# Reversed order inside each group of an attention context's products

## The chip, the cores and the metric

The kernel runs on one core of a Trainium2 chip. The metric is the device time of one execution in microseconds (us). A profile of one execution stands beside the timed runs; its "span" reaches from the first to the last instruction that the profiler recorded, and the execution's own time is a little longer than its span.

Engines are named as in the profile: PE is TensorE's matrix multiplier and PEld its weight load, DVE is VectorE, ACT is ScalarE, POOL is GpSimd, and SP is the engine whose queue starts most transfers. L597 means line 597 of the kernel.

## The reference

For each of 16 batches, x is 512 channels by 1024 tokens, and the mask `cond_2048` holds 0 or 1 per token.

```python
xt = jnp.transpose(x, (0, 2, 1))
q = xt @ Wq.T
qh = q.reshape(B, T, NH, dk).transpose(0, 2, 1, 3)          # 8 heads of 64
scores = scale * jnp.einsum('bhqd,bhkd->bhqk', qh, qh)
logits = (scores * cmask + (1.0 - cmask) * NEG) * rmask
attn = jax.nn.softmax(logits, axis=-1)
ctx = jnp.einsum('bhqk,bhkd->bhqd', attn, qh)
out = ctx.transpose(0, 2, 1, 3).reshape(B, T, D) @ Wo.T
return x + jnp.transpose(out, (0, 2, 1))
```

Queries, keys and values are the same projection. A token with mask 0 is left out as a key; as a query its logits are all zero, so its row of the context is the mean over all tokens.

## The kernel before

**Slots.** About half of the tokens have mask 1. The kernel numbers the tokens of a batch so that those come first, and does attention on the first 544 slots alone: four blocks of 128 slots (i = 0 to 3) and a tail of 32 (i = 4). All other tokens get the mean row.

**A step.** A batch is worked off in 18 steps, in the order of the list `S`: for each head pair p = 0 to 3 and each block i = 0 to 3 one step, and two steps for the tails of four heads each (`None`). In a step (p, i) the function `scores` runs once per head k of the pair (L580): four f16 matmuls, keys of block i against all 544 queries, into a PSUM tile `pss` of which there are two. ACT takes the exponential (L584) into an SBUF tile `p` of 128 x 544 floats, and adds up the rows on its way; there are nine such tiles.

**The context's products.** `attend(b, p, i, ps)` multiplies the block's values by its exponentials and adds the product to the PSUM tile `pav` (L597). It goes over two halves g of the 544 columns and over the two heads k. Each product has 64 output rows, and the two heads lie on different halves of the array's columns and of `pav`'s partitions. The operands are float32, and the profile shows each such product as two matmul rows: 16 batches x 4 pairs x 4 blocks x 2 halves x 2 heads are 1024 products, and 2048 rows. The tail's product (L600) has all 128 output rows and closes the sum; then ACT copies `pav` out (L604), after which the next pair may use the only `pav` tile.

**Groups.** `attend` isn't called in the step of its exponentials. The lists `todo`, `ready` and `now` in `run` hold it back: blocks 0 and 1 of pair p come in step (p, 3), and blocks 2 and 3 in step (p+1, 1), for the last pair in step (0, 1) of the next batch, there with the tail behind them. Two blocks make a group of eight products, or 16 rows of L597. There are eight groups in a batch and 128 in all. Below they are counted from 0: group 0 of a batch is blocks 0 and 1 of pair 0, group 1 is blocks 2 and 3 of pair 0, and so on to group 7.

**What else PE does.** While a batch's attention runs, `run` spreads over its steps the transposes of the next batch's rows (L398), its projection (L421), its values (L467, L484), the row maxima (L509, L518), the transposes of the sums' reciprocals (L633), and the output projection of the batch before (L680). Each piece has a cost, and a step is given pieces until its share of the batch's total is reached. Where the first of them is dear, they are written ahead of the group in the same step, else behind it.

**What sets the order.** The order in which `run` writes the work is a priority and not the final order. When the program is built, a planner goes through all engines with an estimate of each instruction's time; on each engine it takes the first instruction, in the order written, whose operands and buffers are ready by its estimate. The order that comes out is fixed, and every engine then works its queue off in that order. The semaphore waits are added after that, and a wait is written only where the engine hasn't waited already for the same or a later point of the other engine.

Of the kernel before, what the change touches and what calls it, by code (L numbers as in the profile page):

```python
# [49 lines left out]
class Fast:  # L50
# [537 lines left out]

    def attend(self, b, p, i, ps):
        nc, s = self.nc, self.st[b]  # L590
        if i == 0:
            s["pav"] = self.ps_av.tile([P, 2, 512], F32, tag="av", name="pav")
        for g in range(2):
            for k in range(2):
                cols = slice(g * CH, (g + 1) * CH)
                if i < 4:
                    nc.tensor.matmul(s["pav"][k * DK:(k + 1) * DK, g, :CH], lhsT=s["v"][p][:, i, k * DK:(k + 1) * DK],  # L597
                                     rhs=ps[k][:, cols], start=(i == 0), stop=False)
                else:
                    nc.tensor.matmul(s["pav"][:, g, :CH], lhsT=s["vt"][p // 2][:, k, p % 2 * 2:p % 2 * 2 + 2, :],  # L600
                                     rhs=s["pt"][:, p % 2, cols], start=False, stop=(k == 1))
        if i == 4:
            c = self.sb([P, C], F32, "c", 3)
            nc.scalar.copy(c.rearrange("p (g c) -> p g c", g=2), s["pav"][:, :, :CH])  # L604
            s["c"].append(c)
# [194 lines left out]
    def run(self, flag):  # L800
# [80 lines left out]
        todo, ready, whole = [], [], []  # L881
        for b in range(B + 1):
# [64 lines left out]
            for st, (p, i) in enumerate(S):  # L947
                soon, self.soon = self.soon, []
                for f in soon + free.get(st, []):
                    f()  # L950
                if i is None:
                    self.scores(b, p, None)
                else:
                    ps = [self.scores(b, 2 * p, i)]
                    if i == 2 and whole:
                        whole.pop()()
                    ps.append(self.scores(b, 2 * p + 1, i))

                for _ in range(1 if b < B - 2 else -(-len(self.urgent + self.spare) // (N - st))):
                    self.issue()  # L960
                goal = total * (st + 1) / N
                fill = []
                while pos < len(m) and (done + m[pos][0] / 2 <= goal or st == N - 1):
                    fill.append(m[pos])
                    done += m[pos][0]
                    pos += 1

                big = st >= 4 and [c >= 1 for c, _ in fill if c > 0.1][:1] == [True]
                fill = [f for _, f in fill]

                now = []
                if i in (0, 2):
                    ready, todo = todo, []
                elif i in (1, 3):
                    now, ready = ready, []
                for f in fill + now if big else now + fill:
                    f()
                if i is not None:
                    todo.append(L(self.attend, b, p, i, ps))
                if i == 3:  # L980
                    (whole if p < 3 else todo).append(L(self.attend, b, p, 4, None))
                    if p < 3:
                        free.setdefault(st + 2, []).append(L(self.recip_sums, b, p))
                        free.setdefault(st + 3, []).append(L(self.recip_rows, b, p))
                        if p < 2 or b == B - 1:
                            free.setdefault(st + 5, []).append(L(self.norm, b, p))
# [148 lines left out]
```

## Time and profile before

| | |
|---|---|
| median of 3 runs | 1134.67 us (1131.85 to 1141.19) |
| profiled execution | 1133.56 us |
| its span | 1131.8 us |
| mean granted TensorE clock | 0.992 |
| PE busy | 1090.5 us, 96% |
| PEld busy | 707.9 us, 63% |
| DVE busy | 731.6 us, 65% |
| ACT busy | 676.2 us, 60% |
| POOL busy | 289.1 us, 26% |
| L597, the context's products | 2048 rows, 297.5 us busy |
| L584, the exponentials | 512, 363.3 us busy |

A busy time is the union of an engine's instructions. PE's matmuls overlap, and so the distance from the start of one to the start of the next says more than the duration of one. The idle column of a group of instructions gives the time in which the engine stood still just before them, and what released it.

### The profile page before, as it was taken

What the parts mean: (1) busy time and instruction counts of PE and PEld (TensorE: products, weight loads), DVE (VectorE), ACT (ScalarE), POOL (GpSimd) and SP (SyncE); (2) the same over time, 40 slices, a digit from 0 to 9 for tenths busy, and PEclk for the clock granted to TensorE, in tenths of its full rate; (3) what the DMA queues carried; (4) which work ended last, traced back from release to release, by engine and by line L of the source; (5) the groups of instructions that cost most, each with busy time, mean ns of one, the idle gap of its engine ahead of it and who ended that gap; (6) DMA issues with size and microseconds to landing.
All of it is one profiled execution on the core that took longest, in us unless ns stands there. A gap on an engine that the chain in (4) does not pass through costs nothing.

```text
span 1131.8 us, 23296 instructions
## 1 busy us (share of the span) xinstructions
PE 1090.5 (96%) x8386; PEld 707.9 (63%) x8386; DVE 731.6 (65%) x2369; ACT 676.2 (60%) x1716; POOL 289.1 (26%) x303
## 2 busy tenths in 40 slices
PE   7899999999999999999999999999999999998997
PEld 6566666666666666566666666566666666665543
DVE  6687567675665767667665666856576675655643
ACT  5776666666566666566565665666656566654540
POOL 3101021322202222222222232222222232214642
PEclk9899999999999999999999999999999999999999
DMA  6745554656546454655655566455655654545652
GB/s 212 218 117 151 143 159 128 191 142 179 149 127 175 124 201 137 171 175 158 189 150 165 154 177 185 129 181 144 195 166 156 188 152 130 149 126 174 204 161 77
DMA packets 78122, 181.35 MB, mean 160 GB/s; under 512 B 15008, under 2 KB 16800, under 8 KB 78000
## 3 DMA queue, kind: packets, MB, share of 16 engines
q1 hardware_dynamic: 56816, 111.62, 35.6%
q0 software_dynamic: 21184, 68.18, 18.7%
q8 instruction: 68, 1.11, 0.4%
q14 instruction: 54, 0.44, 0.1%
HBM read 92.34 MB, written 33.91 MB: 112 GB/s over the span
## 4 chain that ended last, share of the span: by engine, by line
PE 66%; DVE 14%; DMA 11%; issue 5%; ACT 2%; POOL 1%; SPq 1%; DVEq 0%; POOLq 0%; ACTq 0%
PE pav L597 19%; PE pss L580 16%; PE pm L680 13%; PE pm L421 8%; DMA rb<-rd 4%; PE pm L398 2%; DMA rd<-rr 2%; PE pav L600 2%; DMA xi<-x_in,idx 2%; PE pm L467 1%; DVE c L664 1%; DMA xx<-hl 1%; PE pm L633 1%; DVE tmp L458 1%; PE pss L555 1%
## 5 line engine op out<-in xcount | busy, mean ns | idle before, releaser
L584 ACT ACTIVATE p<-pss,nm 128x544 f32<-128x544 f32 x512 | 363.3, 714 | 231.5 <-PE pss L580 219.5
L580 PE MATMUL pss<-xx 128*128 128x272 f16 x2048 | 303.0, 281 | 4.2 <-DMA xx<-hl 2.7
L597 PE MATMUL pav<-p,v 128*64 128x272 f32 x2048 | 297.5, 402 | 0.9 <-ACT c L604 0.9
L580 PEld LDWEIGHTS <-xx 128*128 128x128 f16 x2048 | 192.1, 99 | 85.4 <-issue 41.2
L597 PEld LDWEIGHTS pav<-p,v 128*64 128x64 f32 x2048 | 140.6, 137 | 105.4 <-issue 40.9
L764 POOL DMA_INDIRECT y_out<-xa,idx x68 | 70.9, 1043 | 302.4 <-PE pss L580 163.6
L421 PE MATMUL pm<-xh,wqh 128*128 128x274 f16 (+1 forms) x512 | 143.9, 281 | 0.1
L421 PE MATMUL pm<-xl,wqh 128*128 128x274 f16 (+1 forms) x512 | 143.2, 280 | 0.2 <-DVE xl L359 0.2
L421 PE MATMUL pm<-xh,wql 128*128 128x274 f16 (+1 forms) x512 | 143.3, 280 | 0.0
L313 POOL DMA_INDIRECT xa<-x_in,idx x68 | 70.0, 1029 | 184.6 <-PE pss L580 89.3
L421 PEld LDWEIGHTS <-wqh 128*128 128x128 f16 x1024 | 99.9, 99 | 21.9 <-issue 3.4
L584 ACT ACTIVATION_READ_ACCUMULATOR p<-pss,nm 128x1 f32 x512 | 102.7, 201 | 0.0
L685 DVE SCALAR_TENSOR_TENSOR xa<-pm,xa 128x512 f32<-128x512 f32 x60 | 41.4, 689 | 89.6 <-PE pm L680 89.5
L313 POOL DMA_INDIRECT xi<-x_in,idx x60 | 59.6, 994 | 153.9 <-PE pss L555 53.9
L680 PE MATMUL pm<-woh,ch 128*128 128x512 f16 x240 | 91.0, 379 | 0.3 <-DVE ch L667 0.3
L680 PE MATMUL pm<-woh,cl 128*128 128x512 f16 x240 | 91.1, 379 | 0.1
L680 PE MATMUL pm<-wol,ch 128*128 128x512 f16 x240 | 91.0, 379 | 0.0
L424 ACT ACTIVATE q<-pm 128x272 f32<-128x272 f32 (+1 forms) x128 | 51.0, 398 | 64.0 <-PE pm L421 63.8
L764 POOL DMA_INDIRECT y_out<-xi,idx x60 | 60.9, 1015 | 92.0 <-PE pss L580 72.9
L664 DVE TENSOR_TENSOR c<-c,rb 128x544 f32<-128x544 f32 x64 | 46.2, 722 | 49.2 <-DMA rb<-rd 42.5
L680 PEld LDWEIGHTS <-ch 128*128 128x128 f16 x480 | 46.1, 98 | 41.0 <-DVE ch L667 0.8
L751 DVE TENSOR_TENSOR xi<-xi,ub 128x512 f32<-128x512 f32 (+1 forms) x60 | 40.1, 687 | 40.2 <-DMA xi<-x_in,idx 27.7
(191 smaller groups left out, 1585.5 us busy)
## 6 DMA issues: line engine op xcount, KB each, us to landing
xx<-hl SPq DMA_DIRECT2D x256, 136.0 KB
xm<-x_nat_in SPq DMA_DIRECT2D x56, 512.0 KB
rb<-rd SPq DMA_DIRECT2D x128, 136.0 KB
pt<-c SPq DMA_DIRECT2D x64, 136.0 KB
pt<-p SPq DMA_DIRECT2D x64, 136.0 KB
ub<-ud SPq DMA_DIRECT2D x16, 256.0 KB
xi<-x_nat_in SPq DMA_DIRECT2D x8, 256.0 KB
xa<-x_in,idx POOLq DMA_INDIRECT x68, 4.3
```

Of the source, the lines that this page charges most:

```text
L313: dma = self.nc.gpsimd.indirect_dma_start(out=tile[:n], out_offset=None, in_=self.x, in_offset=bass.IndirectOffsetOnAxis(ap=idx, axis=0))
L398: self.pe = nc.tensor.transpose(pt[:, c, :], x[:n, c * P:(c + 1) * P], self.ident[:n, :n]).ins
L421: self.beat = nc.tensor.matmul(pq, lhsT=w[:, c, e * P:(e + 1) * P], rhs=xx[:, c, cols], start=(k == 0), stop=(k == 3 * DC - 1)).ins
L424: nc.scalar.activation(s["q"][:, e, cols], pq, AF.Copy, scale=1.0 / (SX * SW))
L580: self.beat = nc.tensor.matmul(pt[:, g, :CH], lhsT=xx[:, 2 * k, i * P:(i + 1) * P], rhs=xx[:, 2 * k + a, g * CH:(g + 1) * CH], start=(a == ...
L584: self.exp = [nc.scalar.activation(t.rearrange("p (g c) -> p g c", g=2), pt[:, :, :CH], AF.Exp, bias=s["nm"][p // HG][:, p % HG:p % HG + 1 ...
L597: nc.tensor.matmul(s["pav"][k * DK:(k + 1) * DK, g, :CH], lhsT=s["v"][p][:, i, k * DK:(k + 1) * DK], rhs=ps[k][:, cols], start=(i == 0), s ...
L664: nc.vector.tensor_tensor(c, c, s["rb"][p], ALU.mult)
L680: nc.tensor.matmul(po[:cols.stop - cols.start], lhsT=a[:, e, cols], rhs=w[:, e, :], start=(e == 0 and k == 0), stop=(e == DC - 1 and k == 2))
L685: self.nc.vector.scalar_tensor_tensor(x, po, 1.0 / (SX * SW), x, ALU.mult, ALU.add)
L751: self.nc.vector.tensor_tensor(x[:n], x[:n], s["ub"][:n], ALU.add)
L764: dma = self.nc.gpsimd.indirect_dma_start(out=self.out, out_offset=bass.IndirectOffsetOnAxis(ap=idx, axis=0), in_=x, in_offset=None)
```

## The change

Two lines decide the order in a group. Where `run` takes a group up, it turns its first two entries round: the younger block (1, or 3) is written ahead of the older one, and the tail, if there is one, stays last. In `attend` the second head is written ahead of the first, in each half g. With the younger block in front, the block that opens `pav` and sets the start flag is 1 in place of 0. The function `last`, which ends the last batch, calls its two remaining blocks in the order as before. No instruction is added or taken away, and shapes, tiles and buffer counts stay.

```diff
     def attend(self, b, p, i, ps):
         nc, s = self.nc, self.st[b]
-        if i == 0:
+
+        if i == 1:
             s["pav"] = self.ps_av.tile([P, 2, 512], F32, tag="av", name="pav")
         for g in range(2):
-            for k in range(2):
+            for k in (1, 0) if i < 4 else range(2):
                 cols = slice(g * CH, (g + 1) * CH)
                 if i < 4:
                     nc.tensor.matmul(s["pav"][k * DK:(k + 1) * DK, g, :CH], lhsT=s["v"][p][:, i, k * DK:(k + 1) * DK],
-                                     rhs=ps[k][:, cols], start=(i == 0), stop=False)
+                                     rhs=ps[k][:, cols], start=(i == 1), stop=False)
...
                 if i in (0, 2):
                     ready, todo = todo, []
                 elif i in (1, 3):
-                    now, ready = ready, []
+                    now, ready = ready[1::-1] + ready[2:], []
                 for f in fill + now if big else now + fill:
                     f()
```

## The prediction

> **What bounds the kernel now.** I read the page's first part first, then its costliest groups, then the list of what PE waited for, and last the timeline around the groups of products.
>
> ```profile
> PE 1090.5 (96%) x8386; PEld 707.9 (63%) x8386; DVE 731.6 (65%) x2369; ACT 676.2 (60%) x1716; POOL 289.1 (26%) x303
> ...
> L584 ACT ACTIVATE p<-pss,nm 128x544 f32<-128x544 f32 x512 | 363.3, 714 | 231.5 <-PE pss L580 219.5
> L597 PE MATMUL pav<-p,v 128*64 128x272 f32 x2048 | 297.5, 402 | 0.9 <-ACT c L604 0.9
> ```
>
> PE is busy 96% of the span. ACT, which makes the exponentials, stood idle 231.5 us ahead of L584, and 219.5 us of that ended with PE's scores (L580): ACT waits for PE, not PE for ACT. Ahead of L597 PE stood idle 0.9 us in the whole span, and what released it was the copy of the last sum (L604), not an exponential.
>
> The list of PE's waits says the same; these are its lines with ACT as the releaser around the products and scores:
>
> ```profile
> PE pav L597 <- ACT c L604: 0.9, 3, 0.3
> PE pss L580 <- ACT p L559: 0.9, 2, 0.5
> PE pss L580 <- ACT p L584: 0.6, 1, 0.6
> ```
>
> So the wait that the new order addresses, a product that waits for an exponential, has no line at all. PE's order is the bound, and a change to the order of PE's work can gain only by what it does to the gaps between instructions.
>
> **What a group costs.** PE's timeline, columns start and duration in us, then engine, line and count:
>
> ```profile
> 504.03 2.05 PE L597 MATMUL pav<-p,v 128*64 128x272 f32 x16
> 506.01 0.66 PE L467 MATMUL pm<-ident,q 128*128 128x128 f32 x4
> ...
> 516.48 0.67 PE L597 MATMUL pav<-p,v 128*64 128x272 f32 x2
> 517.08 0.33 PE L509 MATMUL pm<-ident,smcol 128*128 128x128 f32 x1
> ...
> 523.86 2.05 PE L597 MATMUL pav<-p,v 128*64 128x272 f32 x14
> 525.84 1.10 PE L580 MATMUL pss<-xx 128*128 128x272 f16 x8
> ```
>
> A whole group of 16 rows takes 506.01 - 504.03 = 1.98 us to the next start. The group at 516.48 is broken: one product alone (two rows) takes 0.60, and the other seven later take 525.84 - 523.86 = 1.98, as much as all eight, since the two heads run side by side and the odd one leaves half the array empty. **A group broken so costs 0.60 more.** Going through the whole timeline, I count 88 of the 128 groups whole and 40 broken; the starts-to-next-starts of all L597 runs add up to 287.7 us, where 128 whole groups would take 128 x 1.985 = 254.1. Broken groups cost 33.6 us now. Group 0 of every batch is broken.
>
> **The change, part by part.**
>
> *Instructions.* None is added or removed: 2048 rows of L597 with the same shapes, the heads still in turn. The group's time stays 1.98 whole. The sum over the group goes through the same tile in another order. Cost 0. No DMA, and no instruction of SP, POOL or DVE, is moved by the text of the change.
>
> *Buffers.* A `p` tile is free when both halves of its head are done, that is with the third, fourth, seventh and eighth product of the group. Before and after, one tile comes free at each of these four, only another one. Exponentials that take a freed tile wait for scores that PE runs behind the group, in nearly all groups. Cost 0; if that cover were gone, an exponential would come at most half a group (1.0 us) later, while ACT has 231.5 us of idle time ahead of these.
>
> *The wait on the youngest exponential.* The first product of a group now needs the youngest of its four exponentials, not the oldest. I compared, for all 128 groups, the start of the first product with the end of that exponential (the 512 L584 pairs in order). For group 0 of batch 7:
>
> ```profile
> 511.81 0.71 ACT L584 ACTIVATE p<-pss,nm 128x544 f32<-128x544 f32 x1
> ...
> 512.41 0.20 ACT L584 ACTIVATION_READ_ACCUMULATOR p<-pss,nm 128x1 f32 x1
> ```
>
> It ended at 512.61, and the product started at 516.48: 3.87 us to spare. In 126 groups the margin is positive, 0.89 us at the least (the last group of the run) and 7.2 in the median. It has to be so: only two `pss` tiles exist, and before nearly every group PE has already run scores into the tiles that the youngest exponentials had to empty. That order also tells the planner that they are done, so a first product that filled a gap before can fill it still. Only groups 0 and 1 of batch 0 start before their youngest exponential ends:
>
> ```profile
> 42.69 0.67 PE L597 MATMUL pav<-p,v 128*64 128x272 f32 x2
> 42.97 0.19 ACT L584 ACTIVATION_READ_ACCUMULATOR p<-pss,nm 128x1 f32 x1
> ...
> 53.86 0.67 PE L597 MATMUL pav<-p,v 128*64 128x272 f32 x2
> ...
> 55.19 0.24 ACT L584 ACTIVATION_READ_ACCUMULATOR p<-pss,nm 128x1 f32 x1
> ```
>
> By the traces' finer times they are 0.48 and 1.58 us early. If PE stood still for both, that is +2.06 us. Behind the waiting product stand the next scores (L580), and for them ACT. From the other side: group 0 is broken in pieces of 0.60, 0.61 and 1.52 us, together 2.73, and group 1 in 0.61, 0.61, 0.61 and 1.06, together 2.89. A product held back until all is ready could leave both whole: 0.75 and 0.91 saved, -1.66. I take the middle, +0.2: PE has other rows at hand in both places (L555, L398), so neither end is likely.
>
> For a queue that can't pass its head the Trainium skill speaks against this change: "TensorE: Matmul & The Clock Gate", section "Part 3: Packing small matmuls — row/col tiling", says that matmuls start and end strictly in the order given, so a youngest operand in front holds back all that stands behind it. By that rule alone the term is the upper end, +2.06; by the rows the planner moves other work in front and it is less. No run here shows a matmul that passed another.
>
> *The plan behind batch 0.* The order that the planner finds for batch 0 shifts by less than 2 us, and all later batches are planned on from there. How far may that carry? I cut the timeline at each batch's first score and counted matmuls. Batches with the same count do the same work: with 506 rows the batches 4, 9, 12 and 13 take 65.78, 65.79, 66.56 and 65.67 us; with 507, 3 and 7 take 66.50 and 66.12; with 518, 5 and 8 take 69.04 and 69.23; with 522, 6 and 10 take 68.53 and 68.91. Batches 3 and 7 have the same order of lines to the last matmul, and so have 5 and 8, and 9, 12 and 13: the plan falls back into the same few patterns after each disturbance. Equal work differs by 0.19 to 0.89 us. If all 15 later batches moved one way by the largest, it would be 15 x 0.89 = 13.4 us, up or down; at random, with about 0.5 each, it is 0.5 x √15 = 2 us. I take 0, nearest to the equal patterns, and keep -13.4 and +13.4.
>
> **The sum.** 1133.56 (the profiled execution, 1.8 above its span) + 0 + 0 + 0.2 + 0 = 1133.8. The median of the three runs lies 1.1 above the profiled execution, which makes 1134.9 against it; I forecast the middle, **1134.3 us**.
>
> **The rivals.**
>
> *Groups close up (faster).* Was the gap-filling first product the planner's mistake, and does the new order keep it from being taken alone? All 16 groups 0 whole would give 16 x 0.60 = 9.6 us, 1124.7; all 40 whole would give 33.6, 1100.7. For it: what the change looks like is a group that starts only when all of it can go. Against it: at 15 of these 16 places the youngest exponential was over 3.6 us old, or ordered so by the scores, and the new first product is as free to slip ahead as the old one. Over 1% faster takes 19 mended groups.
>
> *More groups break (slower).* The plan of batch 0 shifts, later gaps fall elsewhere, and the first product of groups 2 to 7, which are mostly whole, slips alone into them at 0.60 each. Batch 14 shows that it happens: its groups 4, 5 and 7 are broken. It decides from 19 newly broken groups (11.4 us, 1145.7); 25 of the 88 give 1149.3. Against it stand the patterns that repeat.
>
> *PE stands in batch 0 and nothing is replanned.* +2.06 instead of +0.2: 1136.2, inside the likeliest case.
>
> *The change does not do what it says.* The order turns, but there is no wait on exponentials to save. This is the likeliest case itself.
>
> **How the numbers follow.** No change beyond the plan's small shifts, 1127 to 1142 for the most part: 0.74, with the third rival in it. Groups close up: 0.12. More break: 0.14; the ends of ±13.4 are shared out to these two. One per cent is 11.3 us, about what a measurement of this kernel can tell from no change. The range reaches from 1120 to 1149: it takes in 1134.3 - 13.4 and + 13.4, and leaves out some 0.09 below and 0.11 above. Likeliest alone: 1127 to 1142.
>
> **What would show it.** Right: 88 whole groups within a few, L597 idle for ACT still near 1 us, first products at the same places of the batch pattern from batch 2 on, batches of 65.7 to 69.7 us. Wrong: a wait of L597 on L584 in later batches; the count of whole groups moved by over 15; batches with the same count of matmuls whose time differs by over 1 us from the lists above. What would make me wrong most easily is a plan that settles in another pattern than these.

## The result and the profile after

The changed kernel takes 1120.9 us in the median (1119.63 to 1127.47, six runs), beside 1134.72 for the kernel before: a ratio of 0.9884, with a 95% interval from 0.9853 to 0.9915. The profiled execution took 1119.63 us with a span of 1117.8, and 1133.56 with 1131.8 before. So the spans differ by 14.0 us.

The page of the changed kernel, whose lines from 591 on have moved down by one (L598 is the old L597, L601 the old L600, L605 the old L604, L681 the old L680):

```profile
PE 1071.0 (96%) x8386; PEld 697.7 (62%) x8386; DVE 731.6 (65%) x2369; ACT 676.8 (61%) x1716; POOL 288.6 (26%) x303
...
L584 ACT ACTIVATE p<-pss,nm 128x544 f32<-128x544 f32 x512 | 363.8, 715 | 219.9 <-PE pss L580 209.6
...
L598 PE MATMUL pav<-p,v 128*64 128x272 f32 x2048 | 278.9, 402 | 0.9 <-ACT c L605 0.9
```

PE has the same 8386 matmuls and is busy 19.5 us less; L598 alone went from 297.5 to 278.9 us. The mean of one row is 402 ns as before. What fell is the union of the rows: more of them lie side by side. The idle time ahead of them is 0.9 us as before, with the same releaser. No wait on exponentials was there, and none went.

Group 0 of batch 7, which stood in the prediction with its pieces of 2 and 14 rows, now reads so on PE's timeline (start and duration in us, engine, line, count):

```profile
510.32 0.68 PE L598 MATMUL pav<-p,v 128*64 128x272 f32 x4
510.94 0.33 PE L509 MATMUL pm<-ident,smcol 128*128 128x128 f32 x1
...
517.71 1.60 PE L598 MATMUL pav<-p,v 128*64 128x272 f32 x12
519.24 1.10 PE L580 MATMUL pss<-xx 128*128 128x272 f16 x8
...
525.18 2.05 PE L598 MATMUL pav<-p,v 128*64 128x272 f32 x16
527.17 0.33 PE L634 MATMUL pm<-ident,rcol 128*128 128x128 f32 x1
```

The group is broken at the same place, ahead of L509. But the piece in front now has four rows, that is two products, one of each head. It takes 510.94 - 510.32 = 0.62 us to the next start, where one product alone took 0.60. The other piece, 12 rows, takes 519.24 - 517.71 = 1.53, where seven products took 1.98. A whole group costs 1.99, as before. So a group cut in two costs 0.62 + 1.53 - 1.99 = 0.16 us more than a whole one, where it was 0.60.

Over the whole timeline, 88 groups are whole and 40 broken, the very numbers of before, in 192 pieces for 198. Pieces with an odd number of products went from 80 to 8. From start to next start the products take 270.2 us, and took 287.7.

That is 17.5 us, and the span got 14.0. The same sums by line say where the rest went: scores (L580) 261.9 us for 257.6, values (L467) 48.2 for 45.9, tail scores (L555) 21.9 for 20.9; the other lines together gave back 4. Those 4 us are most likely the clock's and not the order's: the granted clock from 34.7 to 41.5 us, ahead of the first products, was 0.50 in the profile of before and 1.00 in this one. In a second profile of the changed kernel (E5 below), with 0.55 there, the products take 270.8 us, the other lines give back under 1 us, and the span is 9.9 us shorter than before. In PE's list of waits:

```profile
PE pm L467 <- DVE q L427: 6.4, 7, 2.6
...
PE pm L398 <- DVE tmp L487: 3.9, 4, 1.3
...
PE pss L580 <- ACT p L584: 1.9, 4, 0.6
```

These three were 4.1, 1.3 and 0.6 before, and the whole list adds up to 37.2 us for 31.9. A PE that gets through the products sooner waits a little longer for VectorE and for the exponentials in other places. Batch 4 shows it: its products take 16.3 us for 17.2, PE's waits are 1.7 us for 0.7, and the batch takes 65.93 us for 65.78.

### The profile page after: what moved, and what is told of

Read it like the earlier page. It is cut to its first block, busy times and chain, and to the rows that moved or that the text cites. A ratio compares the mean times of both kernels' runs of the same rounds, so it can differ in the third digit from the quotient of the medians.

```text
span 1117.8 us, 23184 instructions
## 1 busy us (share of the span) xinstructions
PE 1071.0 (96%) x8386; PEld 697.7 (62%) x8386; DVE 731.6 (65%) x2369; ACT 676.8 (61%) x1716; POOL 288.6 (26%) x303
## 4 chain that ended last, share of the span: by engine, by line
PE 63%; DVE 14%; DMA 10%; issue 7%; ACT 3%; POOL 2%; SPq 1%; DVEq 0%; POOLq 0%; ACTq 0%
PE pav L598 17%; PE pss L580 16%; PE pm L681 13%; PE pm L421 8%; DMA xi<-x_in,idx 3%; DMA rb<-rd 2%; PE pm L398 2%; PE pav L601 2%; DMA rd<-rr 2%; ACT p L584 2%; POOL y_out L765 2%; PE pm L467 1%; DVE c L665 1%; PE pm L634 1%; DVE tmp L458 1%
## 5 line engine op out<-in xcount | busy, mean ns | idle before, releaser
L580 PE MATMUL pss<-xx 128*128 128x272 f16 x2048 | 303.1, 280 | 5.4 <-DMA xx<-hl 2.6
L598 PE MATMUL pav<-p,v 128*64 128x272 f32 x2048 | 278.9, 402 | 0.9 <-ACT c L605 0.9
L580 PEld LDWEIGHTS <-xx 128*128 128x128 f16 x2048 | 192.4, 99 | 85.2 <-issue 40.2
L598 PEld LDWEIGHTS pav<-p,v 128*64 128x64 f32 x2048 | 131.0, 136 | 98.2 <-issue 38.5
L681 PE MATMUL pm<-woh,ch 128*128 128x512 f16 x240 | 91.1, 380 | 1.0 <-DVE xa L686 1.0
L681 PE MATMUL pm<-woh,cl 128*128 128x512 f16 x240 | 91.0, 379 | 0.0
L681 PE MATMUL pm<-wol,ch 128*128 128x512 f16 x240 | 90.9, 379 | 0.0
L681 PEld LDWEIGHTS <-ch 128*128 128x128 f16 x480 | 46.3, 98 | 41.8 <-issue 1.2
```

Of the source, the lines that this page charges most:

```text
L580: self.beat = nc.tensor.matmul(pt[:, g, :CH], lhsT=xx[:, 2 * k, i * P:(i + 1) * P], rhs=xx[:, 2 * k + a, g * CH:(g + 1) * CH], start=(a == ...
L681: nc.tensor.matmul(po[:cols.stop - cols.start], lhsT=a[:, e, cols], rhs=w[:, e, :], start=(e == 0 and k == 0), stop=(e == DC - 1 and k == 2))
```

## The experiments

Theory A says that the gain comes from where the planner cuts a group. In the fixed order on PE, 67 of the 70 cuts within groups of the kernel before, and 60 of the 64 of the changed kernel, fall directly behind a product of the first head, which lies on the lower half of the array's columns. With the first head leading, such a cut leaves a product without a partner on each side of it. With the second head leading, it falls between pairs. Theory B says that the age of the exponentials does it, as the younger block in front suggests. Theory C says that the plan behind batch 0 happened to fall well. E1 to E4 ran on one chip and share 19 runs of the kernel before (1137.22 us in the median).

**E1, the heads alone.**

```diff
-            for k in range(2):
+            for k in (1, 0) if i < 4 else range(2):
```

> The kernel before with the head order alone turned round (second head first, in each half); blocks 0 and 2 stay in front. Theory A (columns): the gain comes from where the planner cuts a group. It cuts only behind a product of the first head, the lower half of the array's columns; with the second head first, a cut then falls between pairs and no head runs alone. In this kernel's fixed order on PE 88 groups are whole, 40 broken, and pieces with an odd number of products go from 80 to 4; so it should be as fast as the changed kernel or a little better: 1119 to 1123 us, L597 269 us from start to next start. Theory B (age): the gain comes from the youngest exponential in front; block 0 or 2 is still the older one, so half of the gain at most: 1127 to 1135. Theory C (chance): the plan behind batch 0 fell well; any time from 1121 to 1148.

Measured: 1122.21 us, ratio 0.9877 (0.9835 to 0.9919). L597 takes 268.1 us from start to next start, and its line on the page has the busy time of the changed kernel:

```profile
L597 PE MATMUL pav<-p,v 128*64 128x272 f32 x2048 | 278.9, 403 | 0.9 <-ACT c L604 0.9
```

The head order alone has the whole gain.

**E2, the blocks alone.**

```diff
-        if i == 0:
+        if i == 1:
             s["pav"] = self.ps_av.tile([P, 2, 512], F32, tag="av", name="pav")
...
-                                     rhs=ps[k][:, cols], start=(i == 0), stop=False)
+                                     rhs=ps[k][:, cols], start=(i == 1), stop=False)
...
-                    now, ready = ready, []
+                    now, ready = ready[1::-1] + ready[2:], []
```

> The kernel before with the block order alone turned round (blocks 1 and 3 first), heads as before. Theory A (columns): no gain, 1131 to 1138 us; 82 odd pieces, L597 287 to 289 us from start to next start. Theory B (age): most of the gain, since a block is two exponentials younger, 1121 to 1128. Theory C: any time from 1121 to 1148.

Measured: 1137.29 us, ratio 1.0007 (0.9988 to 1.0026), L597 288.7 us. Its line on the page:

```profile
L597 PE MATMUL pav<-p,v 128*64 128x272 f32 x2048 | 298.5, 403 | 0.9 <-ACT c L604 0.9
```

The younger block in front is worth nothing, up or down. The order of lines on PE's timeline differs from that of the kernel before in batch 0 alone; from batch 1 on it is the same, row for row. The same holds for E3 beside the kernel before, and for E1 beside the changed kernel. So a shift in batch 0 leaves no trace behind it, and Theory C falls: the later plan goes by the order of the heads.

**E3, the youngest exponential in front, with the lower half leading.** To the changed kernel:

```diff
-                    ps = [self.scores(b, 2 * p, i)]
+                    ps = [self.scores(b, 2 * p + 1, i)]
                     if i == 2 and whole:
                         whole.pop()()
-                    ps.append(self.scores(b, 2 * p + 1, i))
+                    ps.insert(0, self.scores(b, 2 * p, i))
...
-            for k in (1, 0) if i < 4 else range(2):
+            for k in range(2):
```

> The changed kernel with the scores of the second head computed ahead of those of the first, and the first head's products written first again. So the first product of a group still takes the youngest exponential, but the lower half of the columns leads. Theory A (columns): the gain is gone, 1131 to 1138 us, 82 odd pieces. Theory B (age): as the changed kernel, 1119 to 1124. Theory C: any time from 1121 to 1148.

Measured: 1137.68 us, ratio 0.9991 (0.9968 to 1.0015), L598 287.6 us. Its timeline has the old cut back:

```profile
521.54 0.67 PE L598 MATMUL pav<-p,v 128*64 128x272 f32 x2
522.14 0.33 PE L509 MATMUL pm<-ident,smcol 128*128 128x128 f32 x1
```

Theory B falls: each group takes its exponentials from the youngest on, and the gain is gone. What counts is which half of the columns leads.

**E4, heads apart.** In the kernel before:

```diff
-        for g in range(2):
-            for k in range(2):
+        for g, k in ((0, 0), (1, 0), (0, 1), (1, 1)) if i < 4 else ((0, 0), (0, 1), (1, 0), (1, 1)):
+            if True:
```

> The kernel before with the loop over heads outside that over halves: per block first head twice, then second head twice. It measures what a product costs that has no partner in the other half of the columns. If products run side by side only when neighbours in the queue lie on different halves, a whole group takes 5 slots of 0.4585 us and not 4, 2.44 us for 1.985; with 88 whole groups and as much again in the broken ones that is 40 to 60 us: 1175 to 1195 us. If the price of a broken group is the entry into a group alone, the whole groups stay at 1.985 us and the time at 1131 to 1138.

Measured: 1151.09 us, two runs, ratio 1.0124 (1.0084 to 1.0164), L597 304.0 us from start to next start. Slower, but by 14 us and not by 40 to 60: the expectation was wrong for whole groups. On its timeline:

```profile
107.35 1.13 PE L597 MATMUL pav<-p,v 128*64 128x272 f32 x4
108.42 0.66 PE L398 MATMUL pm<-ident,xa 128*128 128x128 f32 x4
...
496.67 2.10 PE L597 MATMUL pav<-p,v 128*64 128x272 f32 x16
498.70 0.65 PE L555 MATMUL pss<-xx 128*32 128x272 f16 x16
```

A whole group takes 498.70 - 496.67 = 2.03 us, 0.05 more than with the heads in turn. A product need not stand next to its partner in the queue. But the piece of four rows at 107.35 holds two products of the same head, and takes 1.07 us where two of both heads took 0.61 or 0.62. So a piece costs about 0.15 us for its entry (0.153 in the sums below) and 0.4585 us for each product of the head that has more of them in it: one alone 0.61, one of each 0.61, two of one 1.07, four and three 1.98, four and four 1.98. That rule, put on the fixed orders, gives 283.4 us before and 266.0 after, a difference of 17.4; measured were 287.7 and 270.2, a difference of 17.5. The 4 us above the rule in both are a few pieces with a longer distance to the next start, most of them in batches 0, 14 and 15.

E5 to E7 ran together on another chip (the kernel before 1131.98 us, seven runs).

**E5, the changed kernel again.**

> The changed kernel once more, beside the two that follow, on their chip. Ratio to the kernel before 0.984 to 0.992. L598 270 us from start to next start, 88 whole groups.

Measured: 1121.52 us, ratio 0.9895 (0.9866 to 0.9924). L598 takes 270.8 us from start to next start, with 88 whole groups.

**E6, groups kept whole, heads in the old order.** In the kernel before, all products of a group but the first are written at a high priority (HPO is a constant of the kernel, 300):

```diff
                 if i < 4:
-                    nc.tensor.matmul(...)
+                    with ExitStack() as st:
+                        if i not in (0, 2) or (g, k) != (0, 0):
+                            st.enter_context(self.tc.high_priority(offset=HPO))
+                        nc.tensor.matmul(...)
```

> The kernel before, its heads in the old order, but all products of a group other than the first are written at a high priority: once the first has gone, nothing cuts the group. In this kernel's fixed order 127 of 128 groups are whole. If broken groups were the cost (theory A), L597 falls from 288 to 255 us from start to next start. 33 us come free; the change got 14 of the 17.5 us that it saved there, the rest went into new waits of PE, so 22 to 33 us faster here: ratio 0.971 to 0.981, without any turn of the heads. If the head order helped in another way (theory D, the pairing on the chip itself), the ratio stays near 1.00 to 0.99.

Measured: 1110.8 us (1107.23 to 1118.52), ratio 0.9802 (0.9777 to 0.9828). On its page of groups:

```profile
L580 PE MATMUL pss<-xx 128*128 128x272 f16 x2048 | 307.7, 281 | 4.2 <-DMA xx<-hl 2.2 <-ACT p L584 1.6
L600 PE MATMUL pav<-p,v 128*64 128x272 f32 x2048 | 266.3, 401 | 0.2
```

L600 is this kernel's line of the products: 266.3 us busy, 258.1 from start to next start, 29.6 less than in the profile of before. The expectation for it was 255, and 22 to 33 us for the whole; the median run got 21. The profiled run, the slowest of the four with a span of 1116.8 us, shows where the rest went: scores 267.7 us for 257.6, values 51.1 for 45.9, tail scores 24.6 for 20.9, and PE's waits, which are part of such sums, add up to 42.0 us for 31.9. Scores and tail scores come in 424 unbroken stretches for 397: what used to cut the groups is now cut more often and kept waiting itself.

**E7, groups kept whole, heads turned.** The changed kernel with the same priority; the exempt product is that of the leading block and the second head.

```diff
                 if i < 4:
-                    nc.tensor.matmul(...)
+                    with ExitStack() as st:
+                        if i not in (1, 3) or (g, k) != (0, 1):
+                            st.enter_context(self.tc.high_priority(offset=HPO))
+                        nc.tensor.matmul(...)
```

> The changed kernel with the same priority on a group's later products. 127 of 128 groups whole. Theory A: the turn of the heads is worth nothing once groups are whole, so this is within 0.5% of the kernel of the row above, ratio 0.971 to 0.982, L598 255 us. Theory D: faster than that by another 1%.

Measured: 1113.14 us, ratio 0.9837 (0.98 to 0.9874). That is 0.2% from E6, within the 0.5% expected, but the ratio lies just above the expected 0.971 to 0.982. Its interval and that of E6 overlap: once groups are whole, the turn of the heads brings no more that shows. E6 is faster than both kernels of this case. E7 is faster than the kernel before, and its interval only touches that of E5; which of E6 and E7 is the better is not settled.

**E8 and E9, pairs kept, heads in the old order.** Only the second head's product of each pair is written at a high priority, in the kernel before; the changed kernel ran beside it (the kernel before 1133.2 us, seven runs).

```diff
                 if i < 4:
-                    nc.tensor.matmul(...)
+                    with self.tc.high_priority(offset=HPO * k):
+                        nc.tensor.matmul(...)
```

> The kernel before, heads and blocks in the old order; the second head's product of each pair alone is written at a high priority, so that a pair is never cut. In its fixed order 86 groups are whole, 42 broken, all of them between pairs: no odd piece, against 80 before. Theory A (a head that runs alone in a broken piece is the cost): as the changed kernel, ratio 0.984 to 0.992, L597 270 to 274 us from start to next start, with more pieces than before. If the count of pieces or the position of the second head itself were the cost, no gain: 0.997 to 1.004.

> The changed kernel beside the row above, on the same chip: ratio 0.984 to 0.992; theory A has both within 0.4% of each other.

Measured: 1123.44 us and ratio 0.9913 (0.988 to 0.9945) with pairs kept, 1122.18 us and 0.9904 (0.9872 to 0.9937) for the changed kernel. The kernel with pairs kept cuts more than any other, in 207 pieces, and takes 269.5 us for its products from start to next start. Its timeline, for group 0 of batch 7, in three pieces:

```profile
511.25 0.68 PE L598 MATMUL pav<-p,v 128*64 128x272 f32 x4
511.86 0.33 PE L509 MATMUL pm<-ident,smcol 128*128 128x128 f32 x1
...
518.64 0.68 PE L598 MATMUL pav<-p,v 128*64 128x272 f32 x4
519.25 0.29 PE L580 MATMUL pss<-xx 128*128 128x272 f16 x1
519.47 1.14 PE L598 MATMUL pav<-p,v 128*64 128x272 f32 x8
520.54 0.98 PE L580 MATMUL pss<-xx 128*128 128x272 f16 x7
```

The heads stand in the old order, and the gain is that of the change. For E1, E6 and E8 the rule from E4 gives 265.2, 255.1 and 266.4 us; 268.1, 258.1 and 269.5 were measured, again 3 us more. That settles it: the cost was products that ran with the other half of the array empty, and every kernel here that keeps the pairs together is rid of it. How much the time gains by it varies more than that sum: the changed kernel's median was 13.8, 10.5 and 11.0 us below that of the kernel before in its three measurements.

## Why the prediction was right and wrong

The forecast was 1134.3 us with a range of 1120 to 1149, "no change" at 0.74 and "faster by over 1%" at 0.12. The measured 1120.9 lies in the range, at its lower end, and on the side that I held unlikely. That it lies in the range is luck: the step that decided the time was wrong.

**Right: no wait on exponentials.** L597 had none to lose. E2 and E3 show that the age of the operand moves the time by no more than their intervals allow, under 0.4% either way. The size of the term of +0.2 us for the two early groups of batch 0 stays open. In the changed kernel no group starts ahead of its youngest exponential. Its groups 0 and 1 of the run start 1.09 and 2.08 us earlier than before, but its first score starts 2.00 us earlier too, under the higher clock named above. In E5's profile the same kernel starts the two groups 2.91 and 1.92 us later than before.

**Right: the count of whole groups.** 88 before, 88 after, and the 40 broken ones are the same groups: group 0 of all batches, group 7 of the first 15, and nine others.

**Wrong: the step on instructions.** The prediction said of the instructions "the heads still in turn" and "Cost 0". This term was -17.5 us, and the span got 14.0 us shorter in the first profile of the changed kernel, 9.9 in E5's. The price was in the same text: a broken group costs 0.60 more, "since the two heads run side by side and the odd one leaves half the array empty". I took that price as one for being broken. Had I split it, it would have read 0.46 for the product without a partner and about 0.15 for another entry, and the question would have been whether groups break at another product, not whether they break. The rows had the answer to half of that: the pieces of before were 1 and 7, or 1, 2 and 5, again and again. Nearly every cut lay behind a first head's product, and the change turns the heads.

**Wrong: the rival for faster.** It asked for 19 groups mended, and none was mended. The gain came from 40 groups that stayed broken, at a lower price each.

**Mis-sized: the plan behind batch 0.** The ends of ±13.4 us for chance shifts of the plan were the reason that the range reached down far enough. They were not what happened. As E1 to E3 show, the shift of batch 0 did not carry: batches 1 to 15 together take 1023.0 us before, 1024.7 in E2 and 1025.9 in E3, but 1014.3 in E1 and 1013.5 in the changed kernel. Most batches got shorter, though not all: those with 518 matmuls went from 69.04 and 69.23 us to 67.75 and 67.76, batches 9 and 13 (506 matmuls) from 65.79 and 65.67 to 64.95 and 64.79, and batch 4, also with 506, stayed for the waits shown above. A batch that differs by over 1 us from those of the same count was a sign of being wrong that the prediction named, and it came. The measurement fell into the range for another reason than the range was made for.

**Open.** That the planner leaves a group behind a product on the lower half, and almost never behind one on the upper half, was read off the fixed orders; why its estimates let it is not explained. What sets how much of the products' saving PE's other waits take back is not settled either.

## What to carry to other kernels

Where two small matmuls share the array side by side, count the pieces that other work cuts the stream into, and in each piece the products of the fuller half: here these two numbers set the time of the products, and not their count. Where a planner fixes the order, look at which product its cuts fall behind, and keep the pairs, or better the whole groups, together with a priority. Split the price of a pattern into its parts before deciding what a change to the order does to it, and don't take what a change seems made for as its mechanism.

## What the runs showed of the hardware

A product on one half of the columns starts beside one on the other half even where it is not next in the queue. In E4 two products of the first head, four rows, are written ahead of the second head's first, and yet the rows of a whole group start two by two, the first two 0.013 us apart, and the group takes 2.03 us, as do all 88 whole groups of E4 (2.03 to 2.04). In a strict order of starts it would be the 2.44 us of E4's expectation. So the sentence ahead of the prediction that every engine works its queue off in the fixed order does not hold, by these times, for the starts of PE's rows in such a group.

The Trainium skill, "TensorE: Matmul & The Clock Gate", section "Part 3: Packing small matmuls — row/col tiling", which the prediction drew on for a strict order, does not agree with that group; here the measurement decides. The profile does not say which of two rows belongs to which head, so the order is inferred from the times.
